# A Macaron block of two expert layers around attention: queries moved late, keys and values moved ahead of the last expert, biases turned before they are read, and a stage's first layer norms done in place

## The chip, the cores and the metric

The kernel runs on one core of a Trainium2 chip, in fp32. The metric is the device time of one execution in microseconds (us). The kernel before has a median of 2377.03 us in 3 runs (2373.43 to 2378.77). The core's engines are named as in the profile: PE is the matrix engine (PEld its weight loads), DVE the vector engine, ACT the scalar engine, POOL GpSimd, SP the engine whose queue issues nearly all transfers. PSUM, where PE writes, has 8 banks here; a bank is reused only after its reader has finished.

## The reference

The input x is 16 x 512 x 256. Three steps follow each other, each added to x:

```
x = x + 0.5 * ffn(layernorm(x))
x = x + attention(layernorm(x))        # causal, rotary, 16 heads of 64
x = x + 0.5 * ffn(layernorm(x))        # the same weights as the first
```

and `ffn` is a soft mixture of 16 experts with one slot each:

```
o   = q + mha(slot_query, x, x)                    # 16 slots read 512 tokens
h   = layernorm(o) * ln_g + ln_b
u   = silu(h @ W1[e] + b1[e]);  g = silu(h @ Wg[e] + bg[e])
y   = (u * g) @ W2[e] + b2[e]                      # slot e through expert e
out = mha(x, o + y, o + y)                         # tokens read the 16 slots
```

## The kernel before

The three steps are called stage 1, attention and stage 2. Both ffn stages run the same function `ffn(n, ...)`, n = 0 and n = 1, in three phases.

*Slot phase.* A loop over the 16 batches, a step i for each and two steps of run-out. For a batch, `normalized` makes the layer norm h (DVE at line 225 for batches 0 and 1, ACT at line 228 for the others), `width_first` transposes it (PE p_hT, line 236; the two halves are copied out by ACT and DVE), PE forms the slots' scores (p_ds, line 529; DVE takes the maximum nmx, line 531, ACT the exponential, line 534), two steps later PE sums the tokens (p_z, line 565), and once in four batches p_mo (line 579). After the loop p_o (line 335) and its transposes give the slots. The layer norm needs mean and variance (`token_stats`, DVE lines 195 and 196) and their inverse root (`pair_rstd`: a square root on ACT, line 200, and a reciprocal on DVE, line 201, for a pair of batches). The first statistics of a stage stand ahead of the loop. In stage 1, `more_constants` loads the biases; its inner function `pieces`, called `constants()` in step i = 5 ahead of that step's p_z, turns them by PE: p_bcol (line 173) and four transposes p_b1g (line 180), all four in one bank, each followed by DVE's copy out of it (line 182).

*Experts.* A loop over e of 16 experts and three steps of run-out. `hidden(e, 0)` and `hidden(e, 1)` are p_u with W1 and Wg (line 607), `back(e-2)` is p_y with W2 (line 634), `gate(e-1)` transposes (p_raw, line 621; then DVE, ACT, DVE), `onto_slots(e-3)` transposes y (p_f, line 644) and adds it into o2T on DVE. Each weight is a tile of 1 MiB; 8 are loaded in the slot phase, the ring holds 12, and `load.more(3)` at the end of an iteration issues the three of expert e + 4 on SP's queue, each as soon as the tile it replaces has been read. `queries(b)` is the projection of a batch's tokens (p_cq, line 378, 8 matmuls, copied out by ACT and DVE): it depends on nothing in this loop and is put between experts as a filler. Five of the 16 run at the slot phase's end, the other 11 as fillers from e = 2 on. `keys_values` (p_kv, line 657, and DVE, line 660) makes the keys and values of 12 slots at e = 16 and of the last four at e = 18.

*Combine.* Two halves of a batch at a time (j): p_cs (line 715), p_vw (line 704), three steps later p_catT (line 736), four later p_cy (line 746), softmax on DVE, ACT and POOL between.

*Attention* runs 64 units (16 batches x 4 groups of heads) in a software pipeline: in iteration u the scores of unit u + 2 (p_as line 929; DVE's causal maximum line 937; ACT's exponential line 941; DVE's reciprocal of the sums, ars, line 946; DVE's transposes line 964) overlap with the values, sums (p_av line 1017) and output (p_ay line 1033, added to x by DVE, line 1037) of earlier units. `exps((1, 0))` issues the last exponentials of a unit, `leave(u, 0)` the first half of the output.

*Order.* PE's instructions run in the order in which they are written. In the slot loop and in attention the same holds for DVE, ACT, POOL and SP (`manual_schedule`); elsewhere (a stage's head, experts, combine) a scheduler orders these four by its own estimate of the times.

Of the kernel before, what the change touches and what calls it, by code (L numbers as in the profile page):

```python
# [9 lines left out]
F32 = mybir.dt.float32  # L10
AF = mybir.ActivationFunctionType
ALU = mybir.AluOpType
# [3 lines left out]
P = 128  # L16
NB, S, D = 16, 512, 256
NT = S // P
NC = D // P
GB = 4  # L20
PB = 2
# [26 lines left out]
def macaron_kernel(ctx: ExitStack, tc: tile.TileContext, a: dict, out: bass.AP):  # L48
# [19 lines left out]
    def by_width(t):  # L68
        return t.rearrange("p (c s) -> p c s", c=NC)
# [81 lines left out]
    def more_constants(su, later):  # L151

        brow = su.tile([R_ALL, P], F32, tag="brow", name="brow", bufs=1)
        for r, nm in ((R_CBQ, "c_bq"), (R_CBK, "c_bk"), (R_CBV, "c_bv")):
            nc.sync.dma_start(brow[r:r + NC, :], a[nm].rearrange("(c p) -> c p", p=P))
        nc.sync.dma_start(brow[R_B2:R_B2 + NS * NC, :], a["e_b2"].rearrange("e (c p) -> (e c) p", p=P))

        for r, src in ((R_BQ, a["attn_bq"]), (R_BK, a["attn_bkv"][0:AH * DQ])):
            for u in range(2):
                nc.sync.dma_start(  # L160
                    brow[r + u * NHG:r + (u + 1) * NHG, :].rearrange("g (j i) -> g j i", j=HG),
                    src.rearrange("(g j u i) -> g u j i", g=NHG, j=HG, u=2)[:, u])
        nc.sync.dma_start(brow[R_BV:R_ALL, :], a["attn_bkv"][AH * DQ:].rearrange("(c p) -> c p", p=P))
        brs = []
        for k, nm in enumerate(("e_b1", "e_bg")):
            br = (su.tile([NS * NQ, QW], F32, tag="br", name="br0", bufs=1) if k == 0 else
                  later.tile([NS * NQ, QW], F32, tag="hE", name="br1"))
            nc.sync.dma_start(br, a[nm].rearrange("e (q i) -> (e q) i", q=NQ))
            brs.append(br)

        def pieces():
            pt = ps("p_bcol")
            nc.tensor.transpose(pt[:, :R_ALL], brow, ident[:R_ALL, :R_ALL])
            nc.vector.tensor_copy(bcol, pt[:, :R_ALL])
            pt = ps("p_b1g")
            n = NS * NQ
            for k, br in enumerate(brs):
                for l in range(NL):
                    i = k * NL + l
                    nc.tensor.transpose(pt[:, i * n:(i + 1) * n], br.rearrange("r (p l) -> r l p", l=NL)[:, l],  # L180
                                        ident[:n, :n])
                    nc.vector.tensor_copy(b1g[:, k].rearrange("p e (l q) -> p l e q", l=NL)[:, l],
                                          pt[:, i * n:(i + 1) * n].rearrange("p (e q) -> p e q", q=NQ))

        return pieces


    mvs, rstds, shifts = {}, {}, {}

    def token_stats(b, t):  # L190
        g = b // PB
# [51 lines left out]
    def ffn(n, last, ahead=None):  # L243
        with ExitStack() as es:
# [4 lines left out]
            cbo = fs.tile([P, D], F32, tag="cbo", name="cbo")  # L249
            hTs = {}  # L250
            with tc.tile_pool(name=f"early{n}", bufs=1) as ew, tc.tile_pool(name=f"slots{n}", bufs=1) as ss:
                w = {"c_Wq": ss.tile([P, NC, D], F32, tag="c_Wq", name="c_Wq")}

                def for_slots(pool):

# [20 lines left out]
                        nc.sync.dma_start(w[nm], a[nm].rearrange("(c p) f -> p c f", p=P))  # L276
                    nc.sync.dma_start(c_wo, a["c_Wo"].rearrange("(c p) f -> p c f", p=P))
                    nc.sync.dma_start(cbo, a["c_bo"].partition_broadcast(P))
                    nc.vector.tensor_scalar_mul(cbo, cbo, 0.5 / FH)

                    nc.vector.tensor_tensor(rows["sqbo"], rows["sqbo"], rows["dbo"], ALU.add)
                    return wvm, rows

                load = Experts(ew)
                slots_and_experts(n, ss, load, w, for_slots, hTs, kT, vT)
            with tc.tile_pool(name=f"comb{n}", bufs=2) as cp:
                combine(n, cp, hTs, kT, vT, c_wo, cbo, last, ahead)

    class Experts:

# [28 lines left out]
    def slots_and_experts(n, ss, load, w, for_slots, hTs, kT, vT):  # L319
# [5 lines left out]
        wvm, rows = for_slots(gpool)  # L325
# [64 lines left out]
        with tc.tile_pool(name=f"disp{n}", bufs=2) as dp, \  # L390
# [5 lines left out]
            direct = set(range(PB + 1 - n)) | {NB - 1}  # L396

            def width(b):
                hTs[b] = by_width(place(b, f"hT{n}_"))
                for c in range(NC):  # L400
                    width_first(hs[b], b, hTs[b], c)

            if n == 0:
                for g in range(2):
                    pair_stats(g)
                    pair_rstd(g, PB - g)
            else:
                for g in range(2, NB // PB - 1):
                    pair_rstd(g)
            pair_shift(1)  # L410
            for b in range(PB + 1):
                hs[b] = normalized(dp, b, 4)
                if b < PB:
                    width(b)
            if n == 1:
                pair_rstd(NB // PB - 1)
            with tc.manual_schedule(engines={mybir.EngineType.DVE, mybir.EngineType.Activation,
                                             mybir.EngineType.Pool, mybir.EngineType.SP}):
                for i in range(NB + 2):
# [61 lines left out]
                queries(1)  # L481
                gathered(NB // GB - 1, zT, moT, wvm)
                queries(2)
                tail = half_of_slots(1)
        gp.close()
        with tc.tile_pool(name=f"late{n}", bufs=1) as lw, \
                tc.tile_pool(name=f"last{n}", bufs=1, side="right") as rw, \
                tc.tile_pool(name=f"exp{n}", bufs=2) as ep:
            load.late, load.last = lw, rw
            load.more(BUFS - EARLY)  # L490
            for nm in ("c_Wk", "c_Wv"):
                w[nm] = rw.tile([P, NC, D], F32, tag=nm, name=nm)
                nc.sync.dma_start(w[nm], a[nm].rearrange("(c p) f -> p c f", p=P))
            queries(3)
            queries(4)
# [91 lines left out]
    def experts(ep, load, w, hET, oT, kT, vT, fillers):  # L587
# [62 lines left out]
        def keys_values(e0, ne):  # L650

            for dst, wm, r, s in ((kT, w["c_Wk"], R_CBK, 1.0 / math.sqrt(DH)), (vT, w["c_Wv"], R_CBV, 1.0)):
                pk = ps(f"p_kv{r}_{e0}")
                for c in range(NC):
                    at = pk[:, c * ne * NB:(c + 1) * ne * NB]
                    for k in range(NC):
                        nc.tensor.matmul(at, wm[:, k, c * P:(c + 1) * P],
                                         o2T[:, k, e0:e0 + ne].rearrange("p e b -> p (e b)"),
                                         start=(k == 0), stop=(k == NC - 1))
# [23 lines left out]
    def combine(n, cp, qTs, kT, vT, c_wo, cbo, last, ahead):  # L683

        xl, vws, ats, atTs, src = {}, {}, {}, {}, xout if n else xin

# [79 lines left out]
        for j in range(nj + 4):  # L766
# [5 lines left out]
            if j < nj:  # L772
# [43 lines left out]
    def attention(qp, wq, wk, wv, wo, cos, sin, row):  # L816
# [239 lines left out]
        with tc.manual_schedule(engines={mybir.EngineType.DVE, mybir.EngineType.Activation,  # L1056
                                         mybir.EngineType.Pool, mybir.EngineType.SP}):
            for u in range(-2, nu):
# [122 lines left out]
```

## Time and profile before

| | |
|---|---|
| median of 3 runs | 2377.03 us (2373.43 to 2378.77) |
| the profiled execution | 2378.72 us, its span 2377.0 us, granted clock 0.989 |
| stage 1, first p_ds | 23.17 us |
| stage 1's experts, first to last p_u | 185.77 to 283.4 us |
| stage 2, first p_hT | 1984.48 us |
| stage 2's experts, first to last p_u | 2139.76 to 2238.5 us |
| PE busy | 2312.3 us (97%) |
| transfers | 346.76 MB, 146 GB/s on average |

The profile is one execution of the program. A row of a timeline gives the start, the duration, the engine, the line, the operation, the tile written and the tiles read, the shape, how many instructions were merged, and in brackets how long the engine was idle before and which work released it. Matmuls overlap, so the time of one group is best read from its start to the next group's start. Where the granted clock of PE falls, the same matmul takes longer; the column PEclk of the windows shows it.

### The profile page before, as it was taken

How to read it: one execution, taken by the hardware profiler on the slowest of the kernel's cores; microseconds unless marked ns; L12 is line 12 of the kernel's file. 1: busy time of each engine (PE TensorE's matmuls, PEld its weight loads, DVE VectorE, ACT ScalarE, POOL GpSimd, SP SyncE). 2: the span in 40 equal slices, each digit the busy share in tenths (PEclk: the TensorE clock that was granted, in tenths of full speed). 3: DMA queues.
4: the chain of work that ended last, by engine and by line, in shares of the span. 5: the costliest groups of instructions: out<-in, count | busy, mean ns of one | idle time of the engine just before them, and what ended most of it. 6: DMA issues, size and time to landing. Idle time of an engine off the chain costs nothing.

```text
span 2377.0 us, 42201 instructions
## 1 busy us (share of the span) xinstructions
PE 2312.3 (97%) x14496; PEld 1448.8 (61%) x14496; DVE 1744.0 (73%) x4596; ACT 1129.6 (48%) x3045; POOL 1064.8 (45%) x1692
## 2 busy tenths in 40 slices
PE   7999899899999999999999999999999999999899
PEld 5665488456565655555555556565555565765488
DVE  6642288788888888888888888888888874532287
ACT  5643233355455555545545545555555555533233
POOL 2210044555564655565656556465555552210043
PEclk9999999999999999999999999999999999999899
DMA  7739852255554555454645455555545453739734
GB/s 235 222 100 386 347 127 63 45 121 111 116 116 115 117 115 117 108 132 95 137 98 127 104 122 110 120 112 121 115 110 126 101 131 106 233 132 388 304 112 138
DMA packets 159709, 346.76 MB, mean 146 GB/s; under 512 B 38980, under 2 KB 98952, under 8 KB 151304
## 3 DMA queue, kind: packets, MB, share of 16 engines
q1 hardware_dynamic: 158908, 343.53, 54.1%
q8 instruction: 115, 1.88, 0.3%
q14 instruction: 98, 0.80, 0.1%
q10 hardware_dynamic: 588, 0.54, 0.1%
HBM read 148.95 MB, written 29.88 MB: 75 GB/s over the span
## 4 chain that ended last, share of the span: by engine, by line
PE 93%; DVE 2%; DMA 2%; ACT 1%; SPq 1%; issue 1%; POOL 0%; DVEq 0%; ACTq 0%; POOLq 0%
PE p_as L929 13%; PE p_av L1017 12%; PE p_v L890 10%; PE p_ay L1033 9%; PE p_k L868 9%; PE p_q L868 9%; PE p_z L565 5%; PE p_ds L529 5%; PE p_cy L746 5%; PE p_cq L378 4%; PE p_cs L715 2%; PE p_u L607 2%; DMA w<-in_e_Wg_dram 1%; PE p_hT L236 1%; PE p_catT L736 1%; PE p_vw L704 1%
## 5 line engine op out<-in xcount | busy, mean ns | idle before, releaser
L949 POOL TENSOR_SCALAR pr<-pr,ars 128x512 f32<-128x512 f32 (+3 forms) x1024 | 523.5, 532 | 654.4 <-DVE ars L946 654.4
L941 ACT ACTIVATE pr<-pr,amn 128x512 f32<-128x512 f32 (+3 forms) x1024 | 561.5, 550 | 461.9 <-DVE amn L937 461.8
L937 DVE CUSTOM_DVE_ANT_0 pr<-p_as,causal 128x512 f32<-128x512 f32 (+3 forms) x1024 | 434.2, 484 | 97.4 <-PE p_as L929 96.1
L964 DVE STREAM_TRANSPOSE sq<-pr 128x768 f32<-128x768 f32 x441 | 375.7, 906 | 13.1 <-issue 12.0
L929 PE MATMUL p_as<-k,q 32*128 32x512 f32 (+3 forms) x4096 | 331.7, 448 | 3.7 <-POOL k L879 3.6
L1017 PE MATMUL p_av<-prT,v 128*64 128x512 f32 (+3 forms) x2048 | 291.2, 437 | 6.8 <-DMA prT<-sq 5.0
L929 PEld LDWEIGHTS p_as<-k,q 32*128 32x128 f32 x4096 | 179.8, 185 | 131.1 <-issue 51.7
L890 PEld LDWEIGHTS p_v<-wv,ahT 128*128 128x128 f32 x1024 | 190.0, 190 | 98.8 <-issue 46.4
L890 PE MATMUL p_v<-wv,ahT 128*128 128x256 f32 x1024 | 249.2, 387 | 0.0
L1017 PEld LDWEIGHTS p_av<-prT,v 128*64 128x64 f32 x2048 | 139.5, 137 | 164.3 <-issue 139.1
L1033 PE MATMUL p_ay<-wo,aoT 128*128 128x256 f32 x1024 | 238.7, 386 | 0.3 <-ACT aoT L1024 0.3
L868 PE MATMUL p_k<-ahT,wk 128*128 128x512 f32 x512 | 236.9, 605 | 0.0
L868 PE MATMUL p_q<-ahT,wq 128*128 128x512 f32 x512 | 230.5, 593 | 0.2 <-ACT ahT L854 0.2
L1033 PEld LDWEIGHTS p_ay<-wo,aoT 128*128 128x128 f32 x1024 | 189.2, 190 | 31.9 <-ACT aoT L1024 1.1
L941 ACT ACTIVATION_READ_ACCUMULATOR pr<-pr,amn 128x1 f32 x1024 | 191.4, 187 | 0.0
L1024 ACT ACTIVATE aoT<-p_av,bcol 128x512 f32<-128x512 f32 x128 | 88.0, 688 | 179.9 <-PE p_av L1017 179.8
L868 PEld LDWEIGHTS p_k<-ahT,wk 128*128 128x128 f32 x512 | 92.1, 190 | 126.2 <-issue 116.4
L868 PEld LDWEIGHTS p_q<-ahT,wq 128*128 128x128 f32 x512 | 97.2, 190 | 95.8 <-issue 86.8
L693 POOL TENSOR_TENSOR kbd<-kT,own 128x256 f32<-128x256 f32 x32 | 19.7, 618 | 286.2 <-DVE kT L660 249.1
L746 PE MATMUL p_cy<-vw,catT 128*128 128x256 f32 x512 | 123.0, 385 | 3.0 <-ACT catT L738 3.0
L893 ACT COPY v<-p_v 128x512 f32<-128x512 f32 x128 | 73.4, 574 | 104.9 <-PE p_v L890 104.9
L565 PE MATMUL p_z<-atT,h 128*128 128x256 f32 x512 | 118.9, 387 | 0.0
(162 smaller groups left out, 3271.3 us busy)
## 6 DMA issues: line engine op xcount, KB each, us to landing
prT<-sq SPq DMA_DIRECT2D x1008, 160.0 KB
w<-in_e_W_dram SPq DMA_DIRECT2D x64, 1024.0 KB
w<-in_e_Wg_dram SPq DMA_DIRECT2D x32, 1024.0 KB
out_dram<-x SPq DMA_DIRECT2D x64, 256.0 KB
awaya<-sqa SPq DMA_DIRECT2D x25, 512.0 KB
atT<-awaya SPq DMA_DIRECT2D x100, 128.0 KB
xl<-in_attn_x_dram SPq DMA_DIRECT2D x16, 512.0 KB
xl<-out_dram SPq DMA_DIRECT2D x16, 512.0 KB
```

The source lines that it names most:

```text
L529: nc.tensor.matmul(psc, qk[:, k, c * P:(c + 1) * P], hT[:, k, :], start=(k == 0), stop=(k == NC - 1))
L565: nc.tensor.matmul(pz[:, c * 256:(c + 1) * 256].rearrange("p (c g i) -> p c g i", c=NC, g=NSQ), h[:, t, c * P:(c + 1) * P], atT[:, t], sta ...
L746: nc.tensor.matmul(py[:, t * D:(t + 1) * D], atT[:, c, t * P:(t + 1) * P], vws[b][:, c, :], start=(c == 0), stop=(c == NC - 1))
L868: nc.tensor.matmul(pq, self.w[:, k, at:at + P], hTs[self.b][:, k, :], start=(k == 0), stop=(k == NC - 1))
L890: nc.tensor.matmul(pv[:, t * 256:(t + 1) * 256], hTs[b][:, k, (t0 + t) * P:(t0 + t + 1) * P], wv[:, k, hg * HG * DQ:(hg + 1) * HG * DQ], s ...
L929: nc.tensor.matmul(banks[j][:, at:at + w], q[n][j * 32:(j + 1) * 32, i * P:(i + 1) * P], k[n][j * 32:(j + 1) * 32, :w], start=(n == 0), st ...
L937: nc.vector.tensor_tensor_reduce(out=self.at(i, j), in0=banks[j][:, at:at + w], in1=causal[:, S - w:], scale=-1.0 / math.sqrt(DQ), scalar= ...
L941: nc.scalar.activation(self.at(i, j), self.at(i, j), AF.Exp, bias=self.mn[:, i, j:j + 1], scale=-1.0, accum_out=self.rs[:, i, j:j + 1])
L949: nc.gpsimd.tensor_scalar(self.at(i, j), self.at(i, j), self.rs[:, i, j:j + 1], 1.0, ALU.mult, ALU.mult)
L964: nc.vector.transpose(view(self.sq, j * blocks * SQ + dst[0] * SQ, [(blocks * SQ, nh)] + [(s * SQ, n) for s, (_, n) in zip(dst[1:], of)] + ...
L1017: nc.tensor.matmul(po[j * DQ:(j + 1) * DQ, :].rearrange("d (a f) -> d a f", a=NSQ)[:, :, t * SQ:], vs[u][:, t, head * DQ:(head + 1) * DQ], ...
L1033: nc.tensor.matmul(py[:, t * D:(t + 1) * D], oTs[u][:, pair, (t0 + t) * P:(t0 + t + 1) * P], wo[:, hg * (HG // 2) + pair, :], start=(pair ...
```

## The change

1. In `pieces`, the four p_b1g transposes come first, then the four copies. `constants()` is called after that step's p_z instead of ahead of it.
2. The scaling of cbo and the sum sqbo + dbo (two DVE instructions) move from `for_slots` into step i = 3 of the slot loop (`prepared`).
3. c_Wq's tile moves to a pool that lives through combine. In stage 2 its load stands behind five other loads on SP's queue.
4. Stage 1's head: statistics and layer norms of the first pair of batches, and their transposes, stand ahead of the second pair's statistics.
5. The end of attention: the seven `pair_rstd` for batches 0 to 13 move into iteration u = 60 behind `exps((1, 0))`; the layer norms of batches 0 and 1 are made in place of x by DVE in iteration u = 63 (`entered`). The statistics of batch 15 and the last `pair_rstd` move into stage 2's head.
6. In stage 2, batches 0 and 1 (`early`) have their transposed norms in tiles of the loop's own pool, so their queries run in the slot loop, right behind their p_z.
7. Fillers are given out so that they end at e = 14: ten in stage 1 (e = 5 to 14), eight in stage 2 (e = 7 to 14). The last query (`later`) runs in combine at j = 3.
8. `keys_values(0, 12)` moves from e = 16 to e = 14, and `hidden(15)` behind it, to the end of iteration 15. In `keys_values`, both halves' matmuls stand ahead of the two DVE instructions.

```diff
             for k, br in enumerate(brs):
                 for l in range(NL):
                     i = k * NL + l
                     nc.tensor.transpose(pt[:, i * n:(i + 1) * n], br.rearrange("r (p l) -> r l p", l=NL)[:, l],
                                         ident[:n, :n])
+            for k in range(2):
+                for l in range(NL):
+                    i = k * NL + l
                     nc.vector.tensor_copy(b1g[:, k].rearrange("p e (l q) -> p l e q", l=NL)[:, l],
                                           pt[:, i * n:(i + 1) * n].rearrange("p (e q) -> p e q", q=NQ))
...
-                w = {"c_Wq": ss.tile([P, NC, D], F32, tag="c_Wq", name="c_Wq")}
+                w = {"c_Wq": fs.tile([P, NC, D], F32, tag="c_Wq", name="c_Wq")}
...
-                    nc.vector.tensor_scalar_mul(cbo, cbo, 0.5 / FH)
-
-                    nc.vector.tensor_tensor(rows["sqbo"], rows["sqbo"], rows["dbo"], ALU.add)
-                    return wvm, rows
+
+                    def prepared():
+                        nc.vector.tensor_scalar_mul(cbo, cbo, 0.5 / FH)
+
+                        nc.vector.tensor_tensor(rows["sqbo"], rows["sqbo"], rows["dbo"], ALU.add)
+                    return wvm, rows, prepared
...
             def width(b):
-                hTs[b] = by_width(place(b, f"hT{n}_"))
+                if b in entered:
+                    hs[b] = entered.pop(b)
+                    early.append(b)
+                    hT = dp.tile([P, NT, D], F32, tag="h", name=f"hT{n}_{b}", bufs=4).rearrange("p t d -> p (t d)")
+                else:
+                    hT = place(b, f"hT{n}_")
+                hTs[b] = by_width(hT)
...
+            early = []
+            order = [b for b in range(NB) if b not in entered]
             if n == 0:
-                for g in range(2):
-                    pair_stats(g)
-                    pair_rstd(g, PB - g)
-            else:
-                for g in range(2, NB // PB - 1):
-                    pair_rstd(g)
+                pair_stats(0)
+                pair_rstd(0, PB)
+            for b in range(PB):
+                if b not in entered:
+                    hs[b] = normalized(dp, b, 4)
+                width(b)
+            if n == 0:
+                pair_stats(1)
+                pair_rstd(1)
             pair_shift(1)
-            for b in range(PB + 1):
-                hs[b] = normalized(dp, b, 4)
-                if b < PB:
-                    width(b)
+            hs[PB] = normalized(dp, PB, 4)
             if n == 1:
+                for t in range(NT):
+                    token_stats(NB - 1, t)
                 pair_rstd(NB // PB - 1)
...
-                    if i == 5 and n == 0:
-                        constants()
                     if i == NB:
-                        queries(0)
+                        queries(order.pop(0))
...
+                        if b in early:
+                            queries(b)
+                    if i == 3:
+                        prepared()
+                    if i == 5 and n == 0:
+                        constants()
...
-            experts(ep, load, w, hET, oT, kT, vT, [lambda b=b: queries(b) for b in range(5, NB)])
+            experts(ep, load, w, hET, oT, kT, vT, [lambda b=b: queries(b) for b in order[:-1]])
+        return lambda: queries(order[-1])
...
                 pk = ps(f"p_kv{r}_{e0}")
-                for c in range(NC):
-                    at = pk[:, c * ne * NB:(c + 1) * ne * NB]
+                ats = [pk[:, c * ne * NB:(c + 1) * ne * NB] for c in range(NC)]
+                for c, at in enumerate(ats):
                     for k in range(NC):
                         nc.tensor.matmul(at, wm[:, k, c * P:(c + 1) * P],
                                          o2T[:, k, e0:e0 + ne].rearrange("p e b -> p (e b)"),
                                          start=(k == 0), stop=(k == NC - 1))
+                for c, at in enumerate(ats):
                     nc.vector.tensor_scalar(dst[:, c, :, e0:e0 + ne].rearrange("p b e -> p e b"),
...
         for e in range(NS + 3):
-            if e < NS:
+            if e < NS - 1:
                 hidden(e, 0)
                 hidden(e, 1)
...
-            if e >= 2 and fillers:
+            if NS - 1 - e <= len(fillers) and fillers:
                 fillers.pop(0)()
-            if e == NS:
+            if e == NS - 2:
                 keys_values(0, NS - 4)
+            if e == NS - 1:
+                hidden(e, 0)
+                hidden(e, 1)
             if e == NS + 2:
                 keys_values(NS - 4, 4)
             load.more(3)
...
+            if j == 3:
+                later()
             if 0 <= j - 3 < nj:
                 turned(j - 3)
...
                 if new:
                     new.exps((1, 0))
+
+                if u == nu - NHG:
+                    for g in range(NB // PB - 1):
+                        pair_rstd(g)
+                if u == nu - 1:
+                    for g in range(PB):
+                        entered[g] = xs[g]
+                        for t in range(NT):
+                            i = (g % PB) * NT + t
+                            nc.vector.tensor_scalar(xs[g][:, t, :], xs[g][:, t, :], mvs[g // PB][:, i, 0:1],
+                                                    rstds[g // PB][:, i:i + 1], ALU.subtract, ALU.mult)
                 if u >= 0:
                     leave(u, 0)
...
-            for g in range(2):
-                pair_rstd(g)
-            for t in range(NT):
-                token_stats(NB - 1, t)
```

More of the change, by code (lines that the diff above doesn't have):

```diff
@@ L185, in more_constants @@
         return pieces
-    mvs, rstds, shifts = {}, {}, {}
+    mvs, rstds, shifts, entered = {}, {}, {}, {}
     def token_stats(b, t):
@@ L278, in for_slots @@
                     nc.sync.dma_start(cbo, a["c_bo"].partition_broadcast(P))
-                    nc.vector.tensor_scalar_mul(cbo, cbo, 0.5 / FH)
-                    nc.vector.tensor_tensor(rows["sqbo"], rows["sqbo"], rows["dbo"], ALU.add)
-                    return wvm, rows
+                    def prepared():
+                        nc.vector.tensor_scalar_mul(cbo, cbo, 0.5 / FH)
+                        nc.vector.tensor_tensor(rows["sqbo"], rows["sqbo"], rows["dbo"], ALU.add)
+                    return wvm, rows, prepared
                 load = Experts(ew)
-                slots_and_experts(n, ss, load, w, for_slots, hTs, kT, vT)
+                later = slots_and_experts(n, ss, load, w, for_slots, hTs, kT, vT)
             with tc.tile_pool(name=f"comb{n}", bufs=2) as cp:
-                combine(n, cp, hTs, kT, vT, c_wo, cbo, last, ahead)
+                combine(n, cp, hTs, kT, vT, c_wo, cbo, last, ahead, later)
     class Experts:
@@ L324, in slots_and_experts @@
         moT = gpool.tile([P, NC, NB * NS], F32, tag="moT", name="moT")
-        wvm, rows = for_slots(gpool)
+        wvm, rows, prepared = for_slots(gpool)
         oT = ss.tile([P, NC, NS, NB], F32, tag="oT", name="oT")
@@ L480, in slots_and_experts @@
                         hs[ahead] = normalized(dp, ahead, 4)
-                queries(1)
+                queries(order.pop(0))
                 gathered(NB // GB - 1, zT, moT, wvm)
-                queries(2)
+                queries(order.pop(0))
                 tail = half_of_slots(1)
@@ L493, in slots_and_experts @@
                 nc.sync.dma_start(w[nm], a[nm].rearrange("(c p) f -> p c f", p=P))
-            queries(3)
-            queries(4)
+            queries(order.pop(0))
+            queries(order.pop(0))
             tail()
-            experts(ep, load, w, hET, oT, kT, vT, [lambda b=b: queries(b) for b in range(5, NB)])
+            experts(ep, load, w, hET, oT, kT, vT, [lambda b=b: queries(b) for b in order[:-1]])
+        return lambda: queries(order[-1])
     class Squares:
@@ L681, in experts, with combine @@
             load.more(3)
-    def combine(n, cp, qTs, kT, vT, c_wo, cbo, last, ahead):
+    def combine(n, cp, qTs, kT, vT, c_wo, cbo, last, ahead, later):
         xl, vws, ats, atTs, src = {}, {}, {}, {}, xout if n else xin
```

## The prediction

> **What bounds the kernel now.** I read the page's first and fourth parts, then TensorE's timeline at each of the two expert stages' ends and heads, then the table of windows, and last DVE and ACT where attention ends.
>
> ```profile
> PE 2312.3 (97%) x14496; PEld 1448.8 (61%) x14496; DVE 1744.0 (73%) x4596; ACT 1129.6 (48%) x3045; POOL 1064.8 (45%) x1692
> PE 93%; DVE 2%; DMA 2%; ACT 1%; SPq 1%; issue 1%; POOL 0%; DVEq 0%; ACTq 0%; POOLq 0%
> ```
>
> PE is 93% of the chain of waits. Only about 65 us of the 2377.0 us span are not PE, so what can be gained are gaps in PE, and matmuls that run slowly after them. Four places have such gaps.
>
> Place 1, stage 1's biases (PE timeline: start, us, engine, line, tile, count, idle before and its releaser):
>
> ```profile
> 55.71 3.62 PE L565 MATMUL p_z<-atT,h 128*128 128x256 f32 x16
> 63.57 0.27 PE L173 MATMUL p_bcol<-ident,brow 62*128 62x62 f32 x1
> 67.75 0.38 PE L180 MATMUL p_b1g<-ident,br 64*128 64x64 f32 x1 [3.80 <-DVE b1g L182]
> 69.14 0.38 PE L180 MATMUL p_b1g<-ident,br 64*128 64x64 f32 x1 [0.32 <-DVE b1g L182]
> 69.45 6.31 PE L565 MATMUL p_z<-atT,h 128*128 128x256 f32 x16
> 75.60 3.60 PE L529 MATMUL p_ds<-hT,qk 128*128 128x512 f32 x8
> ```
>
> Each transpose waits for DVE's copy of the one before; the p_z behind the wait takes 6.31 us, its neighbour 3.62.
>
> Place 2, the end of stage 1's experts; stage 2's is alike, the same rows 1955.2 to 1955.7 us later:
>
> ```profile
> 264.40 3.60 PE L378 MATMUL p_cq<-hT,c_Wq 128*128 128x512 f32 x8
> 267.93 1.93 PE L607 MATMUL p_u<-w,hET 128*32 128x256 f32 x32
> 274.23 1.07 PE L607 MATMUL p_u<-w,hET 128*32 128x256 f32 x16 [1.35 <-DMA w<-in_e_Wg_dram]
> 281.88 1.56 PE L607 MATMUL p_u<-w,hET 128*32 128x256 f32 x16 [0.48 <-DMA w<-in_e_Wg_dram]
> 288.19 0.82 PE L657 MATMUL p_kv<-o2T,c_Wk 128*128 128x192 f32 x4
> 292.98 1.07 PE L634 MATMUL p_y<-w,ug 128*32 128x256 f32 x16
> ```
>
> The last query ends near 267.9. PE then waits for the weights of experts 14 and 15 (7.65 us from one to the next), and the first 12 slots' keys and values stand between the last weights and the last expert's p_y.
>
> The table of windows (us, PE, PEld, DVE, ACT, POOL busy, clock, DMA share, GB/s) says why:
>
> ```profile
> 200.00:204.00 4.00, 4.00 (x18) 2.14 (x14) 1.10 (x4) 0.79 (x3) 0.00 (x0) 1.00 0.92 304
> 2156.00:2160.00 4.00, 4.00 (x38) 1.75 (x40) 0.88 (x2) 0.69 (x1) 0.00 (x0) 1.00 0.89 236
> 2040.00:2060.00 20.00, 20.00 (x86) 13.83 (x85) 9.72 (x20) 12.29 (x28) 5.45 (x17) 1.00 0.88 266
> ```
>
> Most expert windows show about 410 GB/s. The first two rows are dips: early queries held PE back, so buffers came free late. The third is stage 2's slot loop, where PE is never idle.
>
> Places 3 and 4, attention's end and stage 2's head (DVE, ACT, PE timelines):
>
> ```profile
> 1936.12 0.69 DVE L1037 TENSOR_TENSOR x<-p_ay,x 128x512 f32<-128x512 f32 x1
> 1938.07 0.20 DVE L946 RECIPROCAL ars<-ars 128x8 f32<-128x8 f32 x1 [1.26 <-ACT pr L941]
> 1944.86 0.65 DVE L937 CUSTOM_DVE_ANT_0 pr<-p_as,causal 128x512 f32<-128x512 f32 x1
> 1937.55 0.39 ACT L941 ACTIVATE pr<-pr,amn 128x128 f32<-128x128 f32 x1
> 1976.06 1.28 ACT L200 ACT_TABLE_LOAD   x1
> 1984.48 3.91 PE L236 MATMUL p_hT<-ident,h 128*128 128x128 f32 x16 [5.10 <-DVE h L225]
> 1988.18 4.31 PE L529 MATMUL p_ds<-hT,qk 128*128 128x512 f32 x8
> ```
>
> PE idles 5.10 us for stage 2's first layer norms and then runs slowly.
>
> **The sum, stage 1.** *Biases*: 63.57 to 75.60 is 12.03 us. After, p_z runs first (3.5, start to start) and five transposes follow without a wait, 0.11 each (start to start of the first two) or at worst 0.38: 4.0 to 5.4. Saved 6.6 to 8.0; I take -7.4, nearer the back-to-back spacing. *Head*: the first transposes come some 2 us sooner, but on DVE six or seven statistics pairs (about 0.55 each) now stand ahead of the first maximum; -0.3 to +1.5, I take +0.5. *Weights*: without queries in experts 2 to 4 buffers free 3.5 us earlier each; the dip (304 of 410 GB/s for 4 us) is worth 1.0, so -1.0 (0 to -1.7). SP's queue keeps its order; its waits for p_y end sooner, and nothing else is queued behind them. *Experts' end*: from Wg(14) at 274.23 PE now does, back to back, half of p_u 0.9, p_y 1.0, p_raw 0.6, p_f 0.2, a query 3.53, keys and values 3.0 (four groups of 0.75), p_y, p_raw, p_f 1.8, p_u(15) 1.75, p_y(14) 1.0: 288.0. From p_raw to the p_y that needs it took 2.14 before (284.24 to 286.38), so p_y(15) starts at 290.1 instead of 292.98: -2.9. The wait for Wg(15) is gone, but not its whole 6.6: the query and the keys outlast it. Bounds -6.6 (p_y 4.5 us behind the last weights) and 0. *Last keys and values*: one of two DVE waits of 0.42 leaves p_cs's path: -0.4. *Combine*: the last query (3.53) falls on a 2.27 us idle and about 1.3 of slow matmuls: 0 to +1.3, I take +0.2. Stage 1: -11.0.
>
> **Attention.** Seven square roots and two table loads go onto ACT behind its exponentials (end 1938.04); DVE's seven reciprocals stand ahead of the row at 1936.12 and wait. 1938.04 + 1.28 load + 7 x 0.22 (four took 0.88) + 0.3 gives 1941.2; the ars reciprocal of 1938.07 comes near 1942.1, so the causal pass of 1944.86 runs 4.1 late. PE's next p_as at 1945.76 waits for that pass already. +4.1 (0 to +4.5).
> The Trainium skill ("ScalarE: Activation LUTs", What ACT_TABLE_LOAD costs) puts a switch at 2.66 us, with a drain behind the load's 1.28. Here the load of 1976.06 is followed by its square root at 1977.36, which shows no drain; by the page this term would be near +5.5.
>
> **Stage 2.** *Head*: normalisation in place fits DVE's 5.57 us idle before 1977.70, so the transposes follow the last p_ay at 1979.4; p_ds(0) starts near 1981.4, not 1988.18. ACT's two table loads (2.56) then hold the third layer norm back, so of 6.8 I keep -6.0 (-4 to -7). *Early queries*: two, 3.53 each, move from experts paced by DMA into the loop where PE is never idle: +7.1; the cover they had is lost in full. *Weights*: the dip from 2156 to 2160 is worth 4 x (1 - 236/410) = 1.7 at most; -1.5. *Experts' end*: the same chain from Wg(14) at 2229.91 ends 15.9 later at 2245.8 for 2248.19: -2.4. *Keys* -0.4. *Combine*: slow matmuls from 2264.8 to 2270.9 cost about 2, idle 2.27: -0.7. Stage 2: -3.9.
>
> Each late query's two copies go with it to ACT and DVE, which idle over half of an expert (2.30 and 2.73 busy of 12 us from 2224). The moved constants on DVE (0.3 to 0.4 each) and c_Wq's later load cost nothing: the loop leaves DVE half idle (9.72 of 20) and c_Wq's first reader comes steps later; without that cover, under 1 us.
>
> Total -11.0 + 4.1 - 3.9 = -10.8. The profiled execution took 2378.72 (span 2377.0 and 1.7 around it), which is 1.7 above the median of 2377.03. 2378.7 - 10.8 = 2367.9: I say **2368**, own range 2362 to 2372. No change means within 0.2%, 2372.3 to 2381.8.
>
> **Rivals.** *The attention stall stays off PE* (+0 for +4.1): 2364. For it: ACT is idle there until 1939.93. Against: DVE executes in written order. *The ends give nothing*: the last query and the keys push p_y(15) back to its old place (+5.3), perhaps with a stage 2 head of -4 (+2): 2373 to 2375, no change. For it: after Wg(14) PE has no slack. Against: 2.9 us between the two orders' sums. *Slow clock in the experts, slower than before*: with no queries in the early experts PE idles half the time, and once slow, an expert with a query takes 14.1 us instead of 7.06 against 7.65 of DMA, 6.4 late each. From two such experts near the ends (12.9 against 10.8 gained) the kernel is slower; two in each stage are +25.7, so 2394. For it: behind idles of 1.88 and 1.34 p_u took 1.93 at 2229.91, not 1.07. Against: one long run of work ended it there by 2235. The Trainium skill ("TensorE: Matmul & The Clock Gate", Part 1) says an idle window of some 3.4 us halves the clock and as much sustained work restores it; the trace lost it with shorter idles, and by the page's second half the late queries mend themselves.
>
> **How the numbers follow.** Forecast 0.53, stall hidden 0.16, ends give nothing 0.19, slow clock 0.12. The first two are faster by over 0.2%: 0.69; the third is the same: 0.19; the fourth slower: 0.12. The range leaves out the slow clock and a little below: 2360 to 2378.
>
> **What would show it.** p_b1g back to back behind a p_z of 3.6; PE without a DMA wait between Wg(14) and the last p_y, which starts about 16 us behind it; a PE wait of some 4 us at p_as L929, at the place of 1945.76; p_hT within 1 us of the last p_ay; p_cq between the first p_z of stage 2. I am wrong if p_u behind the fillers shows 1.93 for 16, if PE waits for weights throughout both ends, or if the wait in attention is absent.

## The result, and the profile after

The changed kernel takes 2363.09 us (median of 5 runs, 2362.92 to 2366.93) against 2377.03 us of the kernel before (5 runs, 2373.43 to 2378.81). The ratio of the times is 0.9949, with a 95% interval of 0.9935 to 0.9964: faster by half a per cent. The forecast was 2368 us with a range of 2360 to 2378. The profiled execution took 2363.01 us, its span is 2361.3 us, which is 15.7 us less than the span before.

The page of the changed kernel, busy times and shares of the span (most of its line numbers are 3 to 28 higher than those before, up to line 180 they are the same: p_z is L586, p_u L628, p_y L655, p_kv L678):

```profile
PE 2304.5 (98%) x14496; PEld 1439.9 (61%) x14496; DVE 1742.7 (74%) x4596; ACT 1132.5 (48%) x3047; POOL 1067.2 (45%) x1692
```

PE has the same 14496 matmuls as before and is busy 7.8 us less: half of what was gained are waits, the other half matmuls that no longer run at the slow clock. The clock records of the two traces agree: from 25 us to the last matmul PE is granted half its clock for 51 us before, and for 34 after.

The PE timeline of the changed kernel at the biases, at the end of stage 1's experts and in combine (start, us, engine, line, tile, count, wait and its releaser):

```profile
64.65 3.62 PE L586 MATMUL p_z<-atT,h 128*128 128x256 f32 x16
68.20 0.27 PE L173 MATMUL p_bcol<-ident,brow 62*128 62x62 f32 x1
68.31 0.64 PE L180 MATMUL p_b1g<-ident,br 64*128 64x64 f32 x4
68.88 3.70 PE L550 MATMUL p_ds<-hT,qk 128*128 128x512 f32 x8
...
267.71 1.07 PE L628 MATMUL p_u<-w,hET 128*32 128x256 f32 x16 [0.44 <-DMA w<-in_e_Wg_dram]
270.37 3.60 PE L383 MATMUL p_cq<-hT,c_Wq 128*128 128x512 f32 x8
273.80 1.46 PE L678 MATMUL p_kv<-o2T,c_Wk 128*128 128x192 f32 x8
278.39 1.93 PE L628 MATMUL p_u<-w,hET 128*32 128x256 f32 x32
283.26 1.07 PE L655 MATMUL p_y<-w,ug 128*32 128x256 f32 x16 [1.18 <-issue]
295.44 3.60 PE L383 MATMUL p_cq<-hT,c_Wq 128*128 128x512 f32 x8
327.68 1.99 PE L772 MATMUL p_cy<-vw,catT 128*128 128x256 f32 x8 [2.00 <-ACT catT L764]
```

The five transposes of the biases take 0.68 us, behind a p_z of 3.6. Behind Wg(14) (267.71) PE no longer waits for a weight, and the last p_y starts 15.55 us later, where it was 18.75. The last query stands in combine at 295.44, and the wait at p_cy is 2.00 us, with a full-speed p_cy behind it. The kernel before has 2.95 us and 3.78 there:

```profile
338.36 3.78 PE L746 MATMUL p_cy<-vw,catT 128*128 128x256 f32 x8 [2.95 <-ACT catT L738]
```

The same view where attention ends and stage 2 begins, with the rows of ACT and DVE that belong to it:

```profile
1926.65 0.59 DVE L204 RECIPROCAL rstd<-std_g 128x8 f32<-128x8 f32 x3 [3.48 <-ACT std_g L203]
1935.67 1.28 ACT L969 ACT_TABLE_LOAD   x1 [5.98 <-DVE amn L965]
1932.74 0.92 PE L957 MATMUL p_as<-k,q 32*128 32x384 f32 x6
1935.64 1.63 PE L957 MATMUL p_as<-k,q 32*128 32x384 f32 x10 [1.99 <-DVE amn L965]
1937.20 3.56 PE L918 MATMUL p_v<-wv,ahT 128*128 128x256 f32 x8
1967.53 3.29 PE L1061 MATMUL p_ay<-wo,aoT 128*128 128x256 f32 x14 [0.16 <-ACT aoT L1052]
1970.66 1.91 PE L239 MATMUL p_hT<-ident,x 128*128 128x128 f32 x16
1972.41 3.60 PE L550 MATMUL p_ds<-hT,qk 128*128 128x512 f32 x8
1990.83 3.60 PE L383 MATMUL p_cq<-hT,c_Wq 128*128 128x512 f32 x8
2002.03 3.60 PE L383 MATMUL p_cq<-hT,c_Wq 128*128 128x512 f32 x8
```

DVE waits 3.48 us for the roots, PE therefore 1.99 us at p_as, and p_v behind it runs at half speed (3.56 us for 8, where 1.99 is usual). Behind p_v there is no further wait of PE in these two units. Stage 2's transposes follow the last p_ay without any wait, and the two early queries stand in the slot loop.

Where the 15.7 us are, from the start of one row to the start of another, both kernels:

| step | stretch | before | after | difference | predicted |
|---|---|---|---|---|---|
| stage 1's head | start to third p_ds | 34.70 | 35.88 | +1.2 | +0.5 |
| biases | biases (and p_z) to next p_ds | 12.03 | 4.23 | -7.8 | -7.4 |
| weights, stage 1 | first p_u to Wg(14) | 88.46 | 88.56 | +0.1 | -1.0 |
| experts' end, stage 1 | Wg(14) to p_y(15) | 18.75 | 15.55 | -3.2 | -2.9 |
| last keys, stage 1 | p_y(15) to first p_cs | 5.82 | 5.19 | -0.6 | -0.4 |
| combine, stage 1 | first p_cs to first p_as | 130.7 | 127.45 | -3.3 | +0.2 |
| attention | first p_as to last p_ay | 1546.6 | 1551.6 | +5.0 | +4.1 |
| stage 2's head | last p_ay to third p_ds | 22.44 | 15.54 | -6.9 | -6.0 |
| early queries | third p_ds to first p_u | 141.22 | 148.08 | +6.9 | +7.1 |
| weights, stage 2 | first p_u to Wg(14) | 90.15 | 88.46 | -1.7 | -1.5 |
| experts' end, stage 2 | Wg(14) to p_y(15) | 18.28 | 15.56 | -2.7 | -2.4 |
| last keys, stage 2 | p_y(15) to first p_cs | 6.73 | 5.19 | -1.5 | -0.4 |
| combine, stage 2 | first p_cs to last p_cy | 114.54 | 113.41 | -1.1 | -0.7 |

Wg(14) is the second half of p_u of expert 14, which starts when that weight has landed. The change is a sum of gains of some 29 us and of losses of 13 us, 12 of them from two of its parts: the roots in attention and the early queries. Outside the biases, the stretch from the third p_ds to the first p_u of stage 1 takes 139.04 us in both kernels.

### The profile page after: what moved, and what is told of

Its sections match the earlier page's. It is cut to its first block, busy times and chain, and to the rows that moved or that the text cites. A ratio compares the mean times of both kernels' runs of the same rounds, so it can differ in the third digit from the quotient of the medians.

```text
span 2361.3 us, 42200 instructions
## 1 busy us (share of the span) xinstructions
PE 2304.5 (98%) x14496; PEld 1439.9 (61%) x14496; DVE 1742.7 (74%) x4596; ACT 1132.5 (48%) x3047; POOL 1067.2 (45%) x1692
## 3 DMA queue, kind: packets, MB, share of 16 engines
q8 instruction: 115, 1.88, 0.3%
## 5 line engine op out<-in xcount | busy, mean ns | idle before, releaser
L550 PE MATMUL p_ds<-hT,qk 128*128 128x512 f32 x256 | 116.9, 600 | 0.0
```

What stands on the lines that cost most here:

```text
L550: nc.tensor.matmul(psc, qk[:, k, c * P:(c + 1) * P], hT[:, k, :], start=(k == 0), stop=(k == NC - 1))
```

## Experiments

Eight kernels, each against the kernel before on the same chip. The first does one part of the change alone, the next six undo, replace or move one part of the changed kernel, and the last puts four edits together. Medians are of 4 runs (the first of 8). The changed kernel's own five runs lie between 2362.92 and 2366.93 us, so where a median differs from its median by 3 us or less, the stretches of the profiles carry the argument.

**Part 1 alone.** The kernel before, with the four transposes ahead of their copies and the call behind p_z:

```diff
-                    if i == 5 and n == 0:
-                        constants()
...
+                    if i == 5 and n == 0:
+                        constants()
                     ahead = i + 3 if i < 1 else i + 2 if i > 1 else NB
```

> The kernel before with part 1 of the change alone (transposes ahead of their copies, and the call behind the step's p_z). Theory: the whole of the 7.8 us by which the changed kernel gained at this place comes from this part: from the step's first transpose or p_z (63.6 us in the kernel before) to the next p_ds takes 4.2 us in place of 12.0, and the first p_u comes 7.8 us earlier, so about 2369.2 us against 2377.0. Rival: some of it needs the other parts (the freed DVE instructions of part 2, or the new head), or it is lost again in the loop before the experts: less than 5 us at the first p_u.

Measured: 2370.67 us against 2376.93, ratio 0.9972 (0.9962 to 0.9982). The first p_u comes at 178.08 us in place of 185.77, 7.7 earlier. The part is worth its 7.8 us by itself. Some 6 us are left in the time. Between the two profiled executions the stretches behind it differ both ways: from the first p_u to Wg(14) it took 90.38 us in place of 88.46, from there to the last p_y 19.83 in place of 18.75 (20.16 in place of 18.28 in stage 2), and stage 2's head took 1.1 us less. None of this was traced to the part.

**The roots behind the last exponentials.**

```diff
-                if u == nu - NHG:
-                    for g in range(NB // PB - 1):
-                        pair_rstd(g)
...
                 if u + 4 < nu and units[u + 4][1] == 0:
                     enter(units[u + 4][0])
+                if u == nu - 2:
+                    for g in range(NB // PB - 1):
+                        pair_rstd(g)
```

> The changed kernel with the seven inverse roots at the end of iteration u = 62, behind the last exponentials, in place of u = 60. Theory: the PE wait of 1.99 us and the slow matmuls behind it come from DVE waiting for ACT's roots and from the second table load ahead of the next exponential; without them the stretch from p_av (1924.4 us in the changed kernel) to the p_av two units on falls from 29.3 to 24.8 us, 4.5 us, and one table load less stands in stage 2's head: about 2358.6 us against 2363.1 of the changed kernel. Rival 1: the wait is there without the roots (the kernel before waited 0.33 us at the same p_as): no gain. Rival 2: the roots at the later place hold back the layer norms, so that stage 2's first p_hT comes later than 1 us behind the last p_ay and the gain is lost there.

Measured: 2357.13 us, ratio 0.9914 (0.9897 to 0.9930), 6.0 us below the changed kernel. The PE timeline of this kernel at the same p_as and at stage 2's head:

```profile
1934.45 1.57 PE L957 MATMUL p_as<-k,q 32*128 32x384 f32 x16
1935.96 1.99 PE L918 MATMUL p_v<-wv,ahT 128*128 128x256 f32 x8
...
1964.78 3.29 PE L1061 MATMUL p_ay<-wo,aoT 128*128 128x256 f32 x14 [0.16 <-ACT aoT L1052]
1967.90 1.91 PE L239 MATMUL p_hT<-ident,x 128*128 128x128 f32 x16
...
1979.30 3.60 PE L550 MATMUL p_ds<-hT,qk 128*128 128x512 f32 x8
```

The wait is gone, p_v is back at 1.99 us, and from p_av to the p_av two units on it is 24.79 us again (29.25 in the changed kernel). The transposes still follow p_ay at once, and the third p_ds stands 14.5 us behind the last p_ay in place of 15.5: the last pair's root needs no table load of its own any more. So the stall is the roots' doing, 4.5 us, and the head pays 1.0 for the second load. Both rivals fall.

**Copies in place of the early queries.**

```diff
                         if b in early:
-                            queries(b)
+                            qT = by_width(place(b, f"hT{n}_"))
+                            nc.scalar.copy(qT[:, 0, :], hTs[b][:, 0, :])
+                            nc.vector.tensor_copy(qT[:, 1, :], hTs[b][:, 1, :])
+                            hTs[b] = qT
+                            order.insert(b, b)
```

> The changed kernel with stage 2's two early queries replaced by a copy of the transposed norm (half on ACT, half on DVE, as the queries' results were copied), and the queries of batches 0 and 1 given out with the others: ten fillers in stage 2 (e = 5 to 14) in place of eight. Theory: in the slot loop two queries cost their whole PE time, 2 x 3.43 us; in the experts they stand in the wait for weights and cost nothing: 6.9 us less up to the first p_u of stage 2 and no change from there to Wg(14): about 2356.2 us. Rival: ACT and DVE set the pace of those two steps, so that less than 3 us is gained; or ten fillers delay the weights and 2 us or more come back in the experts.

Measured: 2356.44 us, ratio 0.9913 (0.9898 to 0.9927), 6.7 us below the changed kernel. From stage 2's first p_hT to its first p_u it is 153.62 us in place of 160.49, 6.87 less, and from there to Wg(14) 87.64 in place of 88.46. Sixteen matmuls cost all their time where PE is never idle and nothing where it waits for weights; neither ACT and DVE nor the weights answer for it.

**Fillers one expert earlier.**

```diff
-            if NS - 1 - e <= len(fillers) and fillers:
+            if NS - 2 - e <= len(fillers) and fillers:
```

> The changed kernel with the fillers one expert earlier in both stages (stage 1 e = 4 to 13, stage 2 e = 6 to 13). Theory: from Wg(14) on PE never waits for a weight, so the query in e = 14 lies on the path with its whole 3.5 us; without it the last p_y comes 3.5 us earlier behind Wg(14) (12.0 us in place of 15.5, just behind the wait for Wg(15)), in both stages, and Wg(14) itself comes at the same time: about 2356.1 us. Rival: the wait for Wg(15) takes its place, with a slower clock behind the idle time: 0 to 1.5 us in each stage. Other rival: the weights slip by the earlier query, because their buffers come free later: Wg(14) 1 us or more later.

Measured: 2357.95 us, ratio 0.9922 (0.9907 to 0.9937), 5.1 us below the changed kernel. The PE timeline of this kernel at the end of stage 1's experts:

```profile
267.77 1.07 PE L628 MATMUL p_u<-w,hET 128*32 128x256 f32 x16 [0.43 <-DMA w<-in_e_Wg_dram]
270.21 0.38 PE L665 MATMUL p_f<-ident,y 128*128 128x128 f32 x2
271.41 1.54 PE L678 MATMUL p_kv<-o2T,c_Wk 128*128 128x192 f32 x8 [0.81 <-DVE o2T L669]
276.07 1.93 PE L628 MATMUL p_u<-w,hET 128*32 128x256 f32 x32
280.94 1.07 PE L655 MATMUL p_y<-w,ug 128*32 128x256 f32 x16 [1.18 <-issue]
```

The last p_y stands 13.17 us behind Wg(14), in both stages: 2.4 us gained, not 3.5. Neither the theory nor its rival had the wait that takes the place of the query: p_kv follows p_f by 1.2 us, since DVE must first add expert 11's result into o2T, and the query had covered that. No wait for Wg(15) appears, and Wg(14) comes at the same time.

**Stage 1's old head.**

```diff
             if n == 0:
-                pair_stats(0)
-                pair_rstd(0, PB)
+                for g in range(2):
+                    pair_stats(g)
+                    pair_rstd(g, PB - g)
             for b in range(PB):
...
-            if n == 0:
-                pair_stats(1)
-                pair_rstd(1)
```

> The changed kernel with stage 1's head as before (both pairs' statistics and roots ahead of the first layer norms). Theory: the new head brings the first scores forward by 3.8 us but leaves PE 3.47 us without work before the next transposes and runs them at the slow clock, 1.2 us lost at the third p_ds (35.88 against 34.70): undone, the third p_ds comes at 34.7, the first p_u 1.2 us earlier, about 2361.9 us against 2363.1. Rival: the slots' loop has slack of its own for that delay, or the old head now meets other waits: no difference at the first p_u.

Measured: 2361.46 us, ratio 0.9934 (0.9919 to 0.9949). The third p_ds comes at 34.60 us and the first p_u at 177.87 in place of 179.15: 1.3 us, carried through the whole slot loop. Part 4 of the change is a small loss. The changed kernel's PE timeline shows how:

```profile
19.39 3.60 PE L550 MATMUL p_ds<-hT,qk 128*128 128x512 f32 x8
26.46 2.80 PE L239 MATMUL p_hT<-ident,h 128*128 128x128 f32 x8 [3.47 <-ACT h L231]
29.05 5.25 PE L550 MATMUL p_ds<-hT,qk 128*128 128x512 f32 x8
```

The first scores come 3.8 us earlier, but DVE makes seven statistics before the first maximum (23.10); ACT then loads the exponential's table (23.84), makes the exponential (25.14), and only behind it, in its written order, the third layer norm (25.81). PE idles 3.47 us, and the next p_hT and p_ds run slowly (2.80 and 5.25 us for 1.04 and 3.60).

**The last query as a filler.**

```diff
-            experts(ep, load, w, hET, oT, kT, vT, [lambda b=b: queries(b) for b in order[:-1]])
-        return lambda: queries(order[-1])
+            experts(ep, load, w, hET, oT, kT, vT, [lambda b=b: queries(b) for b in order])
+        return lambda: None
```

> The changed kernel with the last query as one more filler (stage 1 e = 4 to 14, stage 2 e = 6 to 14) and none in combine. Theory: the query in combine fills a wait of 2.27 us for POOL, and it shifts ACT's order so that the later wait at p_cy is 2.0 and not 2.95 us, which keeps the clock up: without it the stretch from the first p_cs to attention's first p_as goes back from 127.5 to 130.4 us in stage 1 and that from the first p_cs to the last p_cy from 113.4 to 114.5 in stage 2, in spite of 3.4 us less work in each; the experts' ends stay as they are: about 2367.1 us. Rival: the shorter stretches came from how the clock happened to fall, and the query costs part of its 3.4 us: 2360 to 2363 us.

Measured: 2365.86 us, ratio 0.9952 (0.9937 to 0.9967), 2.8 us above the changed kernel. The PE timeline of this kernel in stage 1's combine and at the same place in stage 2's:

```profile
298.58 0.71 PE L762 MATMUL p_catT<-ident,cat 128*128 128x128 f32 x4 [2.27 <-POOL cat L753]
330.04 3.53 PE L772 MATMUL p_cy<-vw,catT 128*128 128x256 f32 x8 [2.95 <-ACT catT L764]
...
2252.10 0.65 PE L762 MATMUL p_catT<-ident,cat 128*128 128x128 f32 x4 [2.28 <-POOL cat L753]
```

In stage 1 the stretch is back at 130.42 us, as expected (130.4): both waits return to 2.27 and 2.95 us and the slow p_cy with them. In stage 2 the expectation fails: 111.07 us in place of 114.5, and 2.3 less than with the query (113.41). There the wait is 2.28 us as before, but no spell at half clock falls into the stretch, so the rival holds: the query costs most of what lies over the wait. Of the 2.3 us the query itself is 1.0: three other kernels with it and without such a spell there (the late roots, the copies, the four edits) take 0.95 us more than this one. The rest is one spell of 3.41 us at half clock in the changed kernel. The query in combine is worth 3 us in stage 1 and loses 2.3 in stage 2 by these two profiled executions, whose times differ by 1.35 us where the medians differ by 2.8.

**Keys and values back.**

```diff
-            if e < NS - 1:
+            if e < NS:
                 hidden(e, 0)
                 hidden(e, 1)
...
-            if e == NS - 2:
+            if e == NS:
                 keys_values(0, NS - 4)
-            if e == NS - 1:
-                hidden(e, 0)
-                hidden(e, 1)
```

> The changed kernel with the keys and values of 12 slots back at e = 16 and the last expert's hidden part back at the head of its iteration; queries still end at e = 14. Theory: the work of PE behind Wg(14) is the same in both orders, and only waits differ: 0.5 for Wg(15), and 1.2 at p_y(14) that the keys no longer cover, less 0.8 of other cover: the last p_y starts 16.5 us behind Wg(14) in place of 15.55, 1.0 us in each stage, about 2365 us. Rival: the keys in front of the last expert are what the gain of 3.2 us at the experts' end came from: the last p_y 18 us or more behind Wg(14), 2368 us or more.

Measured: 2364.56 us, ratio 0.9945 (0.9928 to 0.9962), 1.5 us above the changed kernel. The PE timeline of this kernel:

```profile
265.89 1.07 PE L628 MATMUL p_u<-w,hET 128*32 128x256 f32 x16 [0.41 <-DMA w<-in_e_Wg_dram]
272.35 1.07 PE L628 MATMUL p_u<-w,hET 128*32 128x256 f32 x16 [0.20 <-DMA w<-in_e_W_dram]
274.79 1.07 PE L628 MATMUL p_u<-w,hET 128*32 128x256 f32 x16 [1.36 <-DMA w<-in_e_Wg_dram]
278.80 1.07 PE L655 MATMUL p_y<-w,ug 128*32 128x256 f32 x16 [1.18 <-issue]
283.29 1.07 PE L655 MATMUL p_y<-w,ug 128*32 128x256 f32 x16
```

The last p_y starts 17.4 us behind Wg(14) in stage 1 and 16.15 in stage 2, 16.8 on average (expected 16.5; changed kernel 15.55). The keys ahead of the last expert are worth 0.6 to 1.9 us in a stage, no more. Stage 1 has the wait of 1.36 us for Wg(15) shown above, and in stage 2 that wait is 0.39.

**Four edits together**: the old head, the late roots, the copies, and the fillers one expert earlier; no new code beside the diffs above.

> The changed kernel with four edits: stage 1's old head, the roots at u = 62, copies in place of the early queries, and the fillers one expert earlier. Theory: the places lie apart, so the gains add: 1.2 + 5.5 + 6.9 + 4.8 = 18.4 us, about 2344.7 us. Rival: ten fillers from e = 4 on in stage 2 and the earlier end of the queries let PE idle and its clock fall at the end of the experts, or the weights slip: 3 us or more of it are given back, 2348 us or more.

Measured: 2343.21 us (2341.45 to 2343.86), ratio 0.9856 (0.9841 to 0.9871): 34 us below the kernel before and some 20 below the changed one. The page of this kernel:

```profile
span 2341.9 us, 42204 instructions
PE 2297.1 (98%) x14496; PEld 1435.9 (61%) x14496; DVE 1743.5 (74%) x4598; ACT 1130.7 (48%) x3047; POOL 1064.6 (45%) x1692
```

The gains add (expected 2344.7): the places lie apart and PE's order ties them in a row. In stage 2 the last p_y of this kernel starts at 2217.14, behind a Wg(14) p_u of 2203.95: 13.19 us, as with the fillers alone.

## Why the prediction was right, point by point

*The sum.* I had -10.8, and the two profiles differ by 15.7. The largest miss is combine in stage 1 (3.5 us more gained than predicted); weights in stage 1 (+1.1), attention and the two heads (0.7 to 0.9 each) and stage 2's last keys (1.1) follow, and some of them cancel. That the total is only 4.9 us off is luck to that extent.

*The bound.* PE's written order carries every delay to the end, so the terms could be added. The profile after agrees: the differences of the table add up to -15.6 of the -15.7 us, and what stage 1's head and biases gave stands unchanged at the first p_u.

*Stage 1's head*: within its range, +1.2 for +0.5. The seven statistics ahead of the first maximum were named; the slow p_hT and p_ds behind the wait of 3.47 us were not.

*Biases*: right, -7.8 for -7.4, and shown by part 1 alone. The whole error is that the transposes took 0.68 us together, not the 1.0 or so that -7.4 allows.

*Experts' end*: right in the step that mattered. The last weights land about 7.65 us behind Wg(14), and a forecast by that wait alone would have been -6.6. The sum of PE's work between them gave -2.9 and -2.4; measured are -3.2 and -2.7. That the query at e = 14 lies on this path is shown by the fillers one expert earlier (2.4 us in each stage), and that moving the keys gains only 0.6 to 1.9 by putting them back. The rival "the ends give nothing" had PE's lack of slack right and its size wrong.

*Early queries*: right, +6.9 for +7.1, and shown: as copies in the loop and queries among the experts they cost nothing.

*Attention*: the mechanism was right and shown by the late roots; of the size, 4.46 us at that place against 4.1, the parts differ. I had DVE's causal pass 4.1 us late and PE waiting for as long. Counted from the p_av ahead of it the pass came 3.1 us late, and PE lost 2.95 up to p_v (1.99 of them in one wait, the rest in the p_as around it) and 1.57 in p_v at half speed. The drift of 0.5 us over the other units is no more than these profiles differ among themselves.
The Trainium skill ("ScalarE: Activation LUTs", What ACT_TABLE_LOAD costs) would have put each switch at 2.66 us. In the changed kernel the load of 1935.67 ends where the exponential begins, at 1936.96, 1.29 us after its start: no drain shows, and the trace's 1.28 was the figure to use.

*Stage 2's head*: right, -6.9 for -6.0; the table load that I charged was worth 1.0 us by the late roots.

*Weights*: -1.0 predicted and nothing measured in stage 1, -1.5 and -1.7 in stage 2. The early dip is filled in both, but in stage 1 one weight came 1.07 us late (8.75 between two Wg in place of 7.67), and took it back. Over all profiles the stretch from the first p_u to Wg(14) is 88.46 to 90.38 us with early fillers (four stretches) and 87.64 to 89.31 with late ones (sixteen), 1.0 us less in the mean (89.65 and 88.65), which one execution need not show.

*Combine in stage 1*: the step that was wrong. I had +0.2 ("the last query (3.53) falls on a 2.27 us idle and about 1.3 of slow matmuls"), and it is -3.3. With the query in combine the wait of 2.27 us is gone and the later wait at p_cy is 2.00 to 2.01 us; it is 2.95 with slow matmuls behind it in the three kernels without the query (the kernel before, part 1 alone, the last query as a filler). That the query does this is shown; by which of the instructions that it puts onto ACT and DVE was not tried. The term that was mis-sized is the slow clock. By the traces' clock records PE is at half clock for 9 to 10 us of this stretch in the three kernels without the query, which take 130.1 to 130.7 us, and for 0 to 6 us in the seven with it, which take 126.1 to 128.8. At 0.4 to 0.5 us for each us at half clock this is the whole difference: the query's own 3.4 us only replace the waits. What one execution gets between 126.1 and 128.8 is how the clock happens to fall.

*Slow clock in the experts*: it occurs and mends itself. In the changed kernel's table of windows, stage 2 before the fillers start, just ahead of the first (its p_cq stands at 2167.81), and at the second of them (us, PE, PEld, DVE, ACT, POOL busy, clock, DMA share, GB/s):

```profile
2156.00:2160.00 4.00, 3.11 (x32) 1.17 (x28) 0.00 (x0) 0.48 (x1) 0.00 (x0) 0.50 1.06 415
2164.00:2168.00 4.00, 2.86 (x39) 1.93 (x40) 0.21 (x1) 0.96 (x2) 0.00 (x0) 1.00 1.05 414
2176.00:2180.00 4.00, 4.00 (x24) 1.47 (x22) 1.32 (x4) 1.08 (x2) 0.00 (x0) 1.00 1.00 393
```

The granted clock falls to 0.50 where PE has no query and is back at 1.00 ahead of the first filler, so the queries are not what restores it. The transfers run at the same pace throughout: no time is lost, and the rival's condition, two fillers at half speed near the end, never comes.

## What to carry to other kernels

Work that depends on nothing belongs where PE waits for transfers, and every piece moved from there into a loop without idle time costs its full length; a copy that frees the buffer may do what the early work was for. When a wait for a transfer is to be filled, add up what stands between the last two transfers: past that sum, each further piece lies on the path itself. A root on ACT in the middle of exponentials was paid by DVE and PE behind it; behind the last exponential it cost nothing here.

## What the runs showed of the hardware

Whether a table load of ACT uses the idle time ahead of it depended on where the wait stands. In the changed kernel ACT idles 5.98 us and loads the exponential's table only when DVE's maximum is there (1935.67): in the trace a semaphore wait of its own stands ahead of the load. At the start of combine in the same kernel the wait is part of the exponential, and the load is long done when the operand comes (ACT timeline):

```profile
284.84 1.28 ACT L749 ACT_TABLE_LOAD   x1
292.02 0.63 ACT L749 ACTIVATE cat<-cat 128x512 f32<-128x512 f32 x1 [5.90 <-DVE cat L748]
```

Of the 44 loads of the changed kernel the 8 with such a separate wait ahead of them waited, and none of the other 36 did. The 1.28 us of 1935.67 delay DVE, which waits 1.95 us for that exponential (0.67 with the late roots); PE, whose p_v runs at half speed meanwhile, shows no wait for them.

The same wait may or may not slow PE down. The wait of 2.0 us at stage 1's p_cy is followed by a p_cy of 1.99 us in the changed kernel, of 2.48 with the late roots, and of 3.23 with all four edits; the wait of 1.99 us in attention by a p_v of 3.56 us for 1.99. An estimate by waits alone is therefore off by up to 1.6 us at each such place. The Trainium skill ("TensorE: Matmul & The Clock Gate", Part 1) puts the limit at an idle window of some 3.4 us; the rows here show slow matmuls behind shorter waits.

The clock records of the ten traces show what decides it. Within one execution the clock changes only at points that lie whole multiples of 3.41 us apart, and their place differs from execution to execution. I cut each trace into these intervals, from 25 us on, and added up PE's idle time in each that ran at full clock. All 52 intervals with 1.88 us of idle time or more were followed by one at half clock, and of the 6676 with less (the longest 1.81 us) only 12 were, with 0.87 to 1.67 us; why those 12 is open. So a wait of 2.0 us within one interval slows the next one (the four edits: 2.01 us idle in the interval ahead of p_cy), and the same wait cut in two by a boundary does not (the changed kernel: 1.77 us idle in the interval ahead of p_cy). Ends of matmuls are modelled in these profiles, so the limit is known to a tenth or two of a microsecond only.
